# A convolution stage's in-order queues: table work in smaller pieces, moments and v's statistics at later steps

## The chip, the cores and the metric

The kernel runs on one core of a Trainium2 chip, in float32. The metric is the device time of one execution in microseconds (us); three executions of the kernel before took 2783.5, 2785.92 and 2796.28 us, with the median at 2785.92. The profile is of one further execution, whose instructions span 2780.5 us.

A core has engines that run beside one another, each through a queue of its own: TensorE (PE, and PEld for its weight loads), VectorE (DVE), ScalarE (ACT), GpSimd (POOL) and SyncE (SP), which here issues nearly all DMA transfers. They wait for one another through semaphores.

## The reference

The input x has 16 images of 16 channels, 256 by 256. There are two layers, each with a group norm ahead and a residual:

```python
x = x + _L0_conv_ref(_gn(x), L0_conv_weight)             # 3x3 circular convolution
x = x + _L1_conv_ref(_gn(x), ty, tx, poles1, poles2, residues)
```

The group norm takes mean and variance over groups of two channels of one image. The first layer is a circular 3x3 convolution, written with Fourier transforms in the reference. The second multiplies the spectrum of its input by tables that are made from complex poles and residues (terms like 1/(i omega - pole) along both axes), transforms back, and adds a transient part built from exp(pole t) and the same poles. The sum of x and the first layer is called v in the kernel; the second layer needs v's group norm, hence v's statistics.

## The kernel before

The program has three stages. The convolution stage reads x, forms v and stores it (vD). A second stage transforms v, mixes channels and stores spectra. A third one transforms back and writes the output. The change is in the first stage alone.

**The convolution stage.** One loop counts steps g from 0 to 386. An image takes 24 steps: four units of six steps, where a unit is a pair of row groups and the six steps are two phases by three taps. `conv(g)` issues 16 matmuls of 32 by 32 weights (32 in the trace) into ps_conv; row groups 2 and 3 run three steps behind 0 and 1. When a unit is complete, ScalarE evicts it into vt with the image's bias (line 266) and sums squares (line 274). VectorE later takes its moments (vst, line 268) and folds it (`mirror`, lines 231 and 232: vsum, then vt in place), and SyncE stores both.

**The row statistics of x** (`x_stats`) run one image ahead, as a generator that yields pairs of a due time and a piece of work. A due time d for image b means: run at step 24b - d. The pieces are sixteen `bn_stats` of x (line 166; the first eight on the image's first half of rows, the others on the second half), the aggregate (line 174), three tiny matmuls that spread a value over the channels of a group (`spread`, line 178, into ps_stat), with VectorE work between them: about_mean (lines 186 to 188), root (lines 194 and 195, the square root is on ScalarE), conv_weights (lines 154 to 157 and 202 to 211) and biases (lines 217 and 218). The buffer xq, which holds the aggregate and the bias, exists twice. ps_stat exists once.

**The loads of x.** Five buffers of half an image each. The first half of image b + 2 is loaded at step 3 of image b, the second at step 15.

**The tables** for the later stages are made beside the convolution by generators, one piece per call. One chain (poles, the two hat tables, the table c) is called at every second step, the other (the exponentials for both axes, then coef) at every fifth step. A hat table is made in two halves: loads from hD, squares on ScalarE (lines 425 and 426), a sum on GpSimd (428), a reciprocal of 512 columns (430), three multiplies on GpSimd (433), three VectorE operations (435, 437, 438), and four pairs of matmuls into ps_setup (448). Table c repeats eight times: GpSimd forms a denominator for two poles (571 to 573), VectorE inverts it (576), GpSimd builds weights (580) and multiplies (594), PE sums (607). An exponential piece: GpSimd forms an angle and its rounded number of turns (495 to 500), VectorE reduces the angle in three steps and clips it (506 to 508), ScalarE takes the sine (510), GpSimd multiplies and folds (512, 514).

**v's statistics** (`v_stats`) of images 0 to 11 are made in the stage as well, as the generator `early`: VectorE forms per-partition means, PE spreads them (line 322), VectorE goes on, PE sums (line 342), VectorE and ScalarE go on (lines 351 to 353), and a Newton step and a reciprocal finish vmr. Both matmuls use ps_stat. The generator is called at every third step from 297 on.

The order on each engine is the order in which this Python program issues the instructions: in a step first `conv(g)`, then `early`, the loads, the row statistics and the tables.

Of the kernel before, what the change touches and what calls it, by code (L numbers as in the profile page):

```python
# [16 lines left out]
B = 16  # L17
# [7 lines left out]
def conv_then_laplace_kernel(ctx: ExitStack, tc: tile.TileContext, a: dict, out: bass.AP):  # L25
# [15 lines left out]
    nc = tc.nc  # L41
# [93 lines left out]
    g128 = load1("g128", [P, P], tp)  # L135
# [23 lines left out]
    def x_stats(b):  # L159


        st = sp.tile([P, C, 6], FP, name="xst", tag="xst")

        def moments(j):
            r0 = 1 + 2 * (j % 8)
            nc.vector.bn_stats(st[:, j, :], halves[b][j // 8][:, r0 : r0 + 2, 1 : N + 1])  # L166

        for j in range(8):
            yield 38 - j, lambda: moments(j)
        for j in range(8, C):  # L170
            yield 33 - j // 2, lambda: moments(j)
        q = sp.tile([P, 12], FP, name="xq", tag="xq")
        mean, pvar, mu, d, e, var, sd, tmp, r, nb, bias = (q[:, j : j + 1] for j in range(11))
        yield 24, lambda: nc.vector.bn_aggr(q[:, 0:2], st)

        def spread(lhs, rhs):
            ps = pst.tile([P, 512], FP, name="ps_stat", tag="ps_stat")
            nc.tensor.matmul(ps[:, 0:1], lhsT=lhs, rhs=rhs, start=True, stop=True)
            return ps[:, 0:1]

        ps = []
        yield 18, lambda: ps.append(spread(g128, mean))

        def about_mean():

            nc.vector.tensor_copy(mu, ps[0])
            nc.vector.tensor_tensor(d, mean, mu, ALU.subtract)
            nc.vector.scalar_tensor_tensor(e, d, d, pvar, ALU.mult, ALU.add)

        yield 17, about_mean  # L190
        yield 14, lambda: ps.append(spread(g128, e))

        def root():
            nc.vector.tensor_scalar(var, ps[1], 1e-5, None, ALU.add)
            nc.scalar.activation(sd, var, AF.Sqrt)

        yield 12, root
        wc = sp.tile([P, 2, 3, 32], FP, name="wc", tag="wc")

        def conv_weights():  # L200
            newton(sd, var, tmp)
            nc.vector.reciprocal(r, sd)
            nc.vector.scalar_tensor_tensor(
                wc.rearrange("p h t m -> p (h t m)"),
                wband.rearrange("p h t m -> p (h t m)"),
                r,
                imask.rearrange("p h t m -> p (h t m)"),
                ALU.mult,
                ALU.add,
            )  # L210
            nc.vector.tensor_scalar(nb, mu, r, -1.0, ALU.mult, ALU.mult)

        yield 9, conv_weights
        yield 5, lambda: ps.append(spread(wsum.rearrange("p c m -> p (c m)"), nb))

        def biases():
            nc.vector.tensor_copy(bias, ps[2])
            nc.vector.tensor_scalar(shift[:, b : b + 1], mu, -1.0, None, ALU.mult)
            ready[b] = wc, bias

        yield 3, biases
# [171 lines left out]
    def make_hat(side):  # L393

        hatT = wp.tile([P, 6 * N], FP, name="hatT", tag="hatT")
        hatT = hatT[:, 0 : 2 * N].rearrange("p (j e t) -> p j e t", j=2, e=2)  # L400
        nc.sync.dma_start(out=hatT, in_=a[f"hatT{side}"])
        om = sw.tile([P, 3], FP, name="s_kcol", tag="s_kcol")
        nc.sync.dma_start(out=om[:, 0:1], in_=a["kcol"])
        om1, om2, scale = (om[:, j : j + 1] for j in range(3))
        to = ((tabE[:, 1:], tabO[:, :C]), (hB[:, 0], hB[:, 1]))[side]
        n = C * C * 2
        for half in range(2):
            tags = "s_re0", "s_re1", "s_pb", "s_im0", "s_im1", "s_den0", "s_den1"
            tiles = [
                sw.tile([P, 2 * n if t == "s_pb" else n], FP, name=t, tag=t)[:, 0:n] for t in tags  # L410
            ]
            pr, npi, m, sq, nb, g, b2 = tiles
            at = slice(half * n, half * n + n)
            for j in range(5):
                nc.sync.dma_start(out=tiles[j], in_=hD[j, side, at].partition_broadcast(P))
            yield
            yield
            if half == 0:
                omega(om1, om1, rd[:, side : side + 1])
                nc.vector.tensor_tensor(om2, om1, om1, ALU.mult)  # L420
                nc.vector.tensor_scalar(scale, cols[:, 17:18], -1.0, 1.0, ALU.mult, ALU.add)
                nc.vector.tensor_tensor(scale, scale, om1, ALU.add)
                nc.vector.tensor_scalar(hatT[:, 1], hatT[:, 1], scale, None, ALU.mult)
            yield
            nc.scalar.activation(g, sq, AF.Square, bias=om2)
            nc.scalar.activation(b2, nb, AF.Square)
            yield
            nc.gpsimd.tensor_tensor(g, g, b2, ALU.add)
            yield
            nc.vector.reciprocal(g, g)  # L430
            yield
            for z in (pr, npi, nb):
                nc.gpsimd.tensor_tensor(z, z, g, ALU.mult)
            yield
            nc.vector.scalar_tensor_tensor(sq, sq, om2, g, ALU.add, ALU.mult)
            yield
            nc.vector.scalar_tensor_tensor(pr, m, om2, pr, ALU.add, ALU.mult)
            nc.vector.scalar_tensor_tensor(npi, m, om2, npi, ALU.subtract, ALU.mult)
            for j, z in ((5, sq), (6, nb)):
                nc.sync.dma_start(out=z[0:1], in_=hD[j, side, at].unsqueeze(0))  # L440
            yield
            yield
            for eo in range(2):
                hv = to[eo].rearrange("p i (m r) -> p i m r", r=2)[:, 8 * half : 8 * half + 8]
                for ri, parts in enumerate(((pr, sq), (npi, nb))):
                    ps = psu.tile([P, 512], FP, name="ps_setup", tag="ps_setup")
                    for j, src in enumerate(parts):
                        nc.tensor.matmul(
                            ps, lhsT=hatT[:, j, eo], rhs=src, start=j == 0, stop=j == 1
                        )  # L450
                    yield
                    nc.scalar.copy(hv[:, :, :, ri], ps.rearrange("p (i m) -> p i m", i=8))
                    yield
# [24 lines left out]
    def make_exps(which):  # L478
# [10 lines left out]
        for q in range(8):  # L489
# [13 lines left out]
            c2 = float(np.float32(1.93500518798828125e-3))  # L503
            c3 = 2 * np.pi - c1 - c2
            for c in (c1, c2, c3):
                nc.vector.scalar_tensor_tensor(th, rn, -float(c), th, ALU.mult, ALU.add)
            nc.vector.tensor_scalar(th, th, phase, 3.1415925, ALU.add, ALU.min)
            nc.vector.tensor_scalar(th, th, -3.1415925, None, ALU.max)
            yield
# [14 lines left out]
    def make_c():  # L524
# [8 lines left out]
        z = space[:, 2 * N : 2 * N + 64].rearrange("p (j k) -> p j k", j=4)  # L533
# [30 lines left out]
        for k0 in range(0, C, 2):  # L564

            at = k0 // 2 % 2
            den = sw.tile([P, 2, N], FP, name="s_cden", tag=f"s_den{at}")
# [5 lines left out]
                nc.gpsimd.tensor_scalar(den[:, j], den[:, j], pr2[:, k : k + 1], None, ALU.add)  # L573
                nc.gpsimd.tensor_scalar(num[:, j], om, nm1, s0[:, k : k + 1], ALU.mult, ALU.add)
            yield
            nc.vector.reciprocal(den, den)
            w = sw.tile([P, 2, 4, 2, 4, 8], FP, name="s_w", tag=f"s_im{at}")
            for odd in range(2):
                for st in range(2):
# [10 lines left out]
                        ALU.mult,  # L590
                    )
            yield
            yield
            nc.gpsimd.tensor_tensor(num, num, den, ALU.mult)
            yield
# [2 lines left out]
            for i0 in range(0, 4, 2):  # L598
                c = c4[:, i0 : i0 + 2]
                ps = psu.tile([P, 2, N], FP, name="ps_setup", tag="ps_setup")  # L600
# [22 lines left out]
    def chain(*gens):  # L623
        for gen in gens:
            yield from gen
# [10 lines left out]
    for b in range(1, B):  # L636
        at_step.setdefault(max(0, 24 * b - 40), []).append((b, x_stats(b)))
    going = []
    tables = (
        (2, 0, chain(make_poles(), make_hat(0), make_hat(1), make_c())),  # L640
        (5, 1, chain(make_exps(0), make_exps(1), make_coef())),
    )
    early = v_stats(0, B - 4, lambda: pst.tile([P, 512], FP, name="ps_stat", tag="ps_stat"))
    for g in range(24 * B + 3):
        conv(g)
        if g > 24 * (B - 4) + 8 and g % 3 == 0:
            next(early, None)
        b, n = divmod(g, 24)
        if b + 2 < B and n == 3:
            halves[b + 2] = [load_x(b + 2, 0)]  # L650
        if b + 2 < B and n == 15:
            halves[b + 2].append(load_x(b + 2, 1))
        for b, gen in at_step.get(g, ()):
            going.append([b, gen, next(gen)])
        for it in list(going):
            while it[2] is not None and g >= 24 * it[0] - it[2][0]:
                it[2][1]()
                it[2] = next(it[1], None)
            if it[2] is None:
                going.remove(it)  # L660
        for every, first, gen in tables:
            if g % every == first:
                next(gen, None)
# [30 lines left out]
    m, n = cols[:, 16:17], cols[:, 17:18]  # L694
# [783 lines left out]
```

## Time and profile before

| | us |
|---|---|
| median of three executions | 2785.92 |
| span of the profile | 2780.5 |
| first convolution matmul starts | 26.1 |
| last convolution matmul ends | 638.2 |
| VectorE busy in the whole span | 1927.2 (69%) |
| PE busy in the whole span | 2614.0 (94%) |

The step at which each image starts on PE gives the images' durations, in us:

| image | 0 | 1 | 2 | 3 | 4 | 5 | 6 | 7 | 8 | 9 | 10 | 11 | 12 | 13 | 14 | 15 |
|---|---|---|---|---|---|---|---|---|---|---|---|---|---|---|---|---|
| us | 37.3 | 46.4 | 38.2 | 36.5 | 53.0 | 37.6 | 33.9 | 38.3 | 35.1 | 36.2 | 35.8 | 35.9 | 50.8 | 40.5 | 29.0 | 27.8 |

VectorE's larger groups in the stage: the moments of x 162.3 us (256 at 678 ns), the two parts of the fold 92.3 and 80.5 us (64 each, at 1442 and 1258 ns), v's moments 42.3 us (64 at 661 ns), the angle reduction's line 506 37.1 us (48 at 772 ns), and the twelve large reciprocals 26.7 us (eight at 3342 ns) and 13.4 us (four at 3338 ns).

A busy share is an average over a stage. To see what a stage waits for, the waits of each engine are read, and for each wait the instruction that stands at the head of the queue; all behind it on that engine waits too.

### The profile page before, as it was taken

What the parts mean: (1) busy time and instruction counts of PE and PEld (TensorE: products, weight loads), DVE (VectorE), ACT (ScalarE), POOL (GpSimd) and SP (SyncE); (2) the same over time, 40 slices, a digit from 0 to 9 for tenths busy, and PEclk for the clock granted to TensorE, in tenths of its full rate; (3) what the DMA queues carried; (4) which work ended last, traced back from release to release, by engine and by line L of the source; (5) the groups of instructions that cost most, each with busy time, mean ns of one, the idle gap of its engine ahead of it and who ended that gap; (6) DMA issues with size and microseconds to landing.
All of it is one profiled execution on the core that took longest, in us unless ns stands there. A gap on an engine that the chain in (4) does not pass through costs nothing.

```text
span 2780.5 us, 93064 instructions
## 1 busy us (share of the span) xinstructions
PE 2614.0 (94%) x39600; PEld 1956.3 (70%) x39600; DVE 1927.2 (69%) x3562; ACT 1524.6 (55%) x3093; POOL 1069.9 (38%) x989
## 2 busy tenths in 40 slices
PE   6878988798999999998999999999989999999998
PEld 3434444355777777775788888888778888888887
DVE  7888999867888888885444444544346667666666
ACT  4667778665666666664455555555434444444443
POOL 1543566502333333334111111111165656565653
PEclk9999999899999999999999999999999999999999
DMA  7777887655665556664666666666799989999995
GB/s 273 269 243 253 281 287 274 227 186 167 243 228 212 212 198 243 228 226 163 193 190 196 190 187 197 196 194 193 201 282 283 291 283 292 285 289 284 286 286 182
DMA packets 481199, 652.82 MB, mean 235 GB/s; under 512 B 51384, under 2 KB 459960, under 8 KB 466832
## 3 DMA queue, kind: packets, MB, share of 16 engines
q1 hardware_dynamic: 479712, 639.65, 71.1%
q8 instruction: 312, 5.11, 0.7%
q0 software_dynamic: 928, 3.02, 0.4%
q10 hardware_dynamic: 144, 4.19, 0.4%
q14 instruction: 103, 0.84, 0.1%
HBM read 367.22 MB, written 279.50 MB: 233 GB/s over the span
## 4 chain that ended last, share of the span: by engine, by line
PE 64%; DVE 13%; DMA 11%; POOL 4%; issue 4%; ACT 2%; SPq 2%; DVEq 0%; ACTq 0%; POOLq 0%
PE ps_mix L1050 16%; PE ps_s L984 9%; PE ps_y L732 8%; PE ps_y L740 8%; DMA yk<-yD 5%; PE ps_conv L249 5%; PE ps_x L775 4%; PE ps_p L1234 4%; PE ps_f L1258 3%; PE ps_f L1259 3%; DMA out_y<-ol 3%; DVE r L1267 2%; DVE xst L166 2%; PE psd L760 1%; SPq L1181 1%
## 5 line engine op out<-in xcount | busy, mean ns | idle before, releaser
L1050 PEld LDWEIGHTS ps_mix<-abd,sg 128*64 128x64 f32 x8192 | 447.7, 138 | 60.6 <-ACT sg L1107 49.0
L249 PE MATMUL ps_conv<-xt,wc 32*32 32x512 f32 x12288 | 463.6, 621 | 25.7 <-issue 22.6
L1050 PE MATMUL ps_mix<-abd,sg 128*64 128x128 f32 x8192 | 478.6, 275 | 8.6 <-ACT yt L1112 8.6
L1198 POOL TENSOR_TENSOR u<-yk 128x512 f32<-128x512 f32 (+1 forms) x268 | 345.4, 1320 | 311.7 <-PE ps_p L1234 204.3
L748 ACT ACTIVATE t<-ps_y,vmr 128x384 f32<-128x384 f32 x512 | 297.6, 582 | 163.0 <-PE ps_y L740 162.9
L249 PEld LDWEIGHTS ps_conv<-xt,wc 32*32 32x32 f32 x12288 | 232.1, 105 | 211.7 <-issue 137.3
L1112 DVE COPY yt<-ps_mix 128x512 f32<-128x512 f32 x128 | 88.5, 692 | 358.9 <-PE ps_mix L1050 232.6
L955 POOL TENSOR_TENSOR w<-v,mcol 128x2048 f32<-128x2048 f32 x32 | 115.6, 3613 | 562.5 <-DVE v L944 541.3
L732 PE MATMUL ps_y<-tabE,vq 128*128 128x256 f32 x1024 | 313.1, 387 | 8.7 <-DVE vq L721 7.1
L740 PE MATMUL ps_y<-tabO,vq 128*128 128x256 f32 x1024 | 305.9, 380 | 0.0
L1112 ACT COPY yt<-ps_mix 128x512 f32<-128x512 f32 x384 | 219.5, 588 | 153.1 <-PE ps_mix L1050 101.2
L1258 PE MATMUL ps_f<-pt,inv 128*128 128x256 f32 x1008 | 300.9, 380 | 0.0
L1259 PE MATMUL ps_f<-hs,ey 128*128 128x256 f32 x1008 | 299.9, 379 | 0.0
L1234 PEld LDWEIGHTS ps_p<-inv,u 128*128 128x128 f32 x2048 | 265.7, 193 | 46.1 <-issue 24.7
L1234 PE MATMUL ps_p<-inv,u 128*128 128x128 f32 x2048 | 279.1, 280 | 9.1 <-POOL u L1202 8.9
L1262 DVE TENSOR_TENSOR r<-ps_f,q 128x256 f32<-128x256 f32 x256 | 107.1, 418 | 249.8 <-ACT q L1261 249.8
L984 PE MATMUL ps_s<-ct,w 64*32 64x256 f32 x8448 | 261.2, 382 | 13.1 <-POOL w L952 12.2
L1107 ACT COPY sg<-ps_s 128x512 f32<-128x512 f32 x248 | 159.7, 645 | 182.8 <-PE ps_s L984 182.7
L1261 ACT COPY q<-ps_f 128x256 f32<-128x256 f32 x256 | 95.4, 373 | 285.1 <-PE ps_f L1259 283.6
L266 ACT ACTIVATE vt<-ps_conv,xq 128x512 f32<-128x512 f32 x256 | 167.2, 680 | 150.6 <-PE ps_conv L249 142.8
L732 PEld LDWEIGHTS ps_y<-tabE,vq 128*128 128x128 f32 x1024 | 189.5, 191 | 85.2 <-ACT q L788 50.3
L1236 ACT COPY pt<-ps_p 128x512 f32<-128x512 f32 x256 | 150.2, 587 | 134.7 <-PE ps_p L1234 119.2
(240 smaller groups left out, 4168.1 us busy)
## 6 DMA issues: line engine op xcount, KB each, us to landing
xt<-in_x SPq DMA_DIRECT2D x31, 2322.0 KB, 10.4
abd<-aD SPq DMA_DIRECT2D x512, 128.0 KB, 2.6
yD<-yt SPq DMA_DIRECT2D x512, 128.0 KB, 2.6
vl<-vD SPq DMA_DIRECT2D x256, 256.0 KB, 4.1
out_y<-ol SPq DMA_DIRECT2D x128, 512.0 KB, 9.4
s<-vD SPq DMA_DIRECT2D x252, 256.0 KB, 6.2
aD<-spec SPq DMA_DIRECT2D x15, 4096.0 KB, 12.5
yk<-yD SPq DMA_DIRECT2D x60, 1024.0 KB, 8.5
```

What stands on the lines that cost most here:

```text
L249: nc.tensor.matmul(acc[r][32 * c : 32 * c + 32], lhsT=ready[b][0][rows, phase, tap], rhs=halves[b][u // 2][rows, q : q + 5 : 4, 2 - tap : ...
L266: nc.scalar.activation(vt[:, r % 2], acc[r], AF.Identity, bias=ready[b][1], **by_sums)
L732: nc.tensor.matmul(ps[:, 0:N], lhsT=vf[:, xo, 0, j], rhs=tabE[:, 0 : i + 2 : i + 1], start=True, stop=False, skip_group_check=True,)
L740: nc.tensor.matmul(ps[:, P : P + N], lhsT=vf[:, xo, 1, j], rhs=tabO[:, i : C + 1 : C - i], start=False, stop=True, skip_group_check=True,)
L748: nc.scalar.activation(t[:, xo, j].rearrange("p l n -> p (l n)"), ps[:, 0:384], AF.Copy, scale=vmr[:, 0, b0 + j, i : i + 1],)
L984: nc.tensor.matmul(ps[odd][32 * iq : 32 * iq + 32, ro], lhsT=w[rows, iq, kk, ro], rhs=ct[rows, iq, kk], start=True, stop=True,)
L1050: nc.tensor.matmul(ps[64 * t : 64 * t + 64, j], lhsT=sg[:, f : f + 2].rearrange("p f m -> p (f m)"), rhs=abd[jq][:, :, 2 * t + cc, 2 * jj ...
L1112: (nc.vector.tensor_copy if m == 3 else nc.scalar.copy)(o, src)
L1198: nc.gpsimd.tensor_tensor(u[:, :, j].rearrange("p b (c n) -> p c b n", c=8), in0, in1, o)
L1234: nc.tensor.matmul(ps[:, at], lhsT=u[:, n], rhs=tab, start=True, stop=True)
L1258: nc.tensor.matmul(ps[:, e], lhsT=tab, rhs=pt[:, e], start=True, stop=False)
L1259: nc.tensor.matmul(ps[:, e], lhsT=ey[:, e], rhs=hs, start=False, stop=True)
```

## The change

The diff moves work between steps. The large reciprocals of the hat tables and of table c are cut into two of 256 columns, one step of their chain apart. The two last VectorE operations of a hat half are put into separate steps. The angle reduction is cut after its second operation, and the exponential chain is called at every fourth step for it. The second half's moments of x come three steps later, the aggregate two, the first spread and about_mean one; the second spread stays. v's statistics are called at six chosen steps in images 12 and 13 in place of every third step. The aim is that no long block of table work stands ahead of a short operation that another engine waits for, and that moments don't stand in the queue before their data are there.

```diff
         for j in range(8, C):
-            yield 33 - j // 2, lambda: moments(j)
+            yield 30 - j // 2, lambda: moments(j)
...
-        yield 24, lambda: nc.vector.bn_aggr(q[:, 0:2], st)
+        yield 22, lambda: nc.vector.bn_aggr(q[:, 0:2], st)
...
-        yield 18, lambda: ps.append(spread(g128, mean))
+        yield 17, lambda: ps.append(spread(g128, mean))
...
-        yield 17, about_mean
+        yield 16, about_mean
         yield 14, lambda: ps.append(spread(g128, e))
...
-            nc.vector.reciprocal(g, g)
-            yield
+            for z in (g[:, 0 : n // 2], g[:, n // 2 :]):
+                nc.vector.reciprocal(z, z)
+                yield
...
             nc.vector.scalar_tensor_tensor(pr, m, om2, pr, ALU.add, ALU.mult)
+            yield
             nc.vector.scalar_tensor_tensor(npi, m, om2, npi, ALU.subtract, ALU.mult)
...
                 nc.vector.scalar_tensor_tensor(th, rn, -float(c), th, ALU.mult, ALU.add)
+                if c == c2:
+                    yield
...
-            nc.vector.reciprocal(den, den)
+            nc.vector.reciprocal(den[:, 0], den[:, 0])
             w = sw.tile([P, 2, 4, 2, 4, 8], FP, name="s_w", tag=f"s_im{at}")
...
             yield
+            nc.vector.reciprocal(den[:, 1], den[:, 1])
             yield
             nc.gpsimd.tensor_tensor(num, num, den, ALU.mult)
...
-        (5, 1, chain(make_exps(0), make_exps(1), make_coef())),
+        (4, 1, chain(make_exps(0), make_exps(1), make_coef())),
...
-        if g > 24 * (B - 4) + 8 and g % 3 == 0:
+        if g - 24 * (B - 4) in (9, 14, 17, 38, 41, 44):
             next(early, None)
```

## The prediction

> **What bounds the kernel now.** I read the page first (it gives the span and the engines), then the busy time by stage, because an average over three stages with different limits says little. In the answer by stretches each row is a stretch in us, then busy time and instruction count of PE, PEld, DVE, ACT and POOL, then the granted TensorE clock:
>
> ```profile
> 0.00:26.11 26.11, 1.69 (x6) 1.51 (x6) 13.88 (x37) 1.49 (x2) 0.19 (x4) 1.00 0.87 334
> 26.11:638.15 612.04, 527.07 (x12703) 265.82 (x12702) 519.75 (x851) 435.39 (x1007) 273.92 (x252) 0.95 0.73 252
> 638.15:2780.50 2142.35, 2085.26 (x26893) 1688.97 (x26892) 1393.57 (x2674) 1087.72 (x2084) 795.80 (x733) 0.99 0.72 229
> ```
>
> The middle row is the convolution stage. Nothing else is touched by the diff, so the 2142 us after it are taken as fixed. In 612.0 us PE works 527.1 (86%) and VectorE 519.7 (85%): neither is saturated. They lose time to each other. 387 steps make 1.58 us a step.
>
> The same view cut at the images (24 steps each) shows where:
>
> ```profile
> 184.46:237.41 52.95, 38.90 (x806) 17.75 (x791) 44.40 (x68) 30.94 (x69) 17.78 (x13) 0.90 0.67 206
> ...
> 418.49:454.29 35.80, 31.98 (x822) 16.01 (x812) 33.40 (x52) 28.57 (x67) 21.14 (x22) 0.95 0.77 275
> ...
> 490.16:540.93 50.77, 34.73 (x827) 16.29 (x807) 45.31 (x81) 28.58 (x66) 31.61 (x36) 0.83 0.61 213
> 540.93:581.38 40.45, 32.12 (x823) 15.91 (x814) 32.66 (x52) 28.62 (x70) 5.82 (x4) 0.92 0.68 227
> ```
>
> Image 11 (second row) is an ordinary one: VectorE works 33.4 of 35.8 us and bounds it. Images 4 and 12 take 15 us more. So the time to win lies in a few disturbed images and not in all sixteen.
>
> Then the waits, each engine alone, from 60 to 582 us (us in total, times, longest). First VectorE's, then PE's:
>
> ```profile
> DVE xst L166 <- DMA xt<-in_x: 18.4, 6, 7.8
> DVE xq L174 <- ACT vt L266: 13.6, 4, 6.1
> DVE vsum L231 <- ACT vt L266: 12.2, 8, 2.6
> DVE s_th L506 <- POOL s_rn L500: 4.0, 2, 2.2
> DVE s_cden L576 <- POOL s_cden L573: 3.1, 2, 2.1
> ```
>
> ```profile
> PE ps_stat L178 <- DVE xq L174: 13.7, 5, 6.5
> PE ps_stat L322 <- DVE xq L194: 10.4, 1, 10.4
> PE ps_stat L178 <- DVE xq L188: 10.3, 3, 6.8
> PE ps_stat L178 <- DVE vmr L353: 5.1, 1, 5.1
> ```
>
> Last the timeline (start, duration, engine, line, what, and in brackets the idle time before it with what ended it), for three of these:
>
> ```profile
> 183.72 1.29 DVE L166 BATCH_NORM_STATS2 xst<-xt 128x6 f32<-128x512 f32 x2 [7.80 <-DMA xt<-in_x]
> 241.12 0.59 DVE L174 BATCH_NORM_AGGREGATE xq<-xst 128x2 f32<-128x96 f32 x1 [6.08 <-ACT vt L266]
> 514.93 0.60 PE L322 MATMUL ps_stat<-vs,g 128*128 128x12 f32 x2 [10.44 <-DVE xq L194]
> ```
>
> The first is the second half of an image that is not yet in SBUF. The second is the aggregate, which overwrites a buffer whose bias ScalarE still needs. The third is v's mean at step 300, which needs the one ps_stat bank, and that bank is read by the root (L194), which stands behind 3 us of sine reduction and other work in VectorE's queue.
>
> **What the Trainium skill says.** "PSUM — Partial Sum Buffer", section "Engine vs sequencer instructions", has the queues of ScalarE, VectorE and GpSimd as strict FIFO, and matmuls starting in program order. The trace agrees: for the 10.44 us ahead of 514.93 no convolution matmul runs, though its data are there. "TensorE: Matmul & The Clock Gate", section "HAM oscillation — how this bites in real kernels", wants no PE gaps above some 3.4 us, or the clock falls. The image with the 10.44 us gap has 0.83, image 6 (274.99 to 308.91, without such a gap) has 1.00; these losses are inside the durations above, so I don't add them again. "Vector Engine (DVE) Microarchitecture Reference", section "5.2 Measured stream behaviour on trn2", gives about 75 ns fixed cost an instruction; I use it once.
>
> **The change, part by part.** Waits by event are from the VectorE timeline.
>
> Second-half moments go 3 steps later (4.7 us). Their load is issued at step 15 of an image and takes 10.4 us (page, part 6); the first moment came 4 steps (6.3 us) after it and now comes 7 steps (11.1 us) after. Of the six waits on loads, four are on second halves: 2.55, 7.80, 0.47 and 4.07 us, 14.9 in sum. Cut by 4.7 each, 3.1 of the 7.8 stays. Gain 12. First halves (1.67 and 1.79) are not helped.
>
> The aggregate goes 2 steps later (3.2 us). It stood at step 0 of the image and needs the evictions that step 2 issues; now it stands behind them. Waits 4.06, 6.08, 0.40 and 3.04 become 0.9, 2.9, 0 and 0: 9.8 saved on paper. But vsum at step 4 needs the same evictions, so part returns as L231 waiting. I credit half: 5.
>
> v's statistics. Before: pieces at steps 9, 12, 15, 18, 21, 24 of image 12, between the row statistics' own uses of the one ps_stat bank (steps 6, 10, 19). Step 12 needs the root, itself at step 12, and the third spread at 19 needs v's read at 21, which stands two steps behind it. Those are the 10.44 and 5.07 us. After: 9, 14, 17 of image 12 and 14, 17, 20 of image 13, and every use of the bank comes two steps behind the last read. Some 15.5 us of PE waiting go. VectorE sets how much of that is time: some 2 us of its work (L351, L353 and the first reciprocal) also moves from image 12 (45.3 busy) to 13 (32.7). With 3 us idle in each, 43.3 + 3 and 34.7 + 3 make 84.0 against 91.2, 7.2 less; the 4.07 and the 3.04 above lie in the same two images and are partly this gain, so I credit 6, not 7.2.
>
> Reciprocals in two halves and sine reduction in two pieces: no work is saved. The half of s_cden needs only the GpSimd work of its own half, so the 3.1 us of waiting go: 3. Shorter blocks in the queue serve the waits on L174 and L188; nothing more credited.
>
> Gains 12 + 5 + 6 + 3 = 26 us.
>
> Costs. Twelve more instructions at 75 ns: 1. The sine chain: its rate stays (4 pieces of 5 steps become 5 of 4), but from one sine to the next reduction there are 12 steps and not 15, 4.7 us less for GpSimd. The timeline's sixteen reductions now have 0 to 24 us between L500's end and L506's start; five have less than 4.7 (0.0, 0.0, 1.3, 3.0, 4.3), which would lack 14.9 in all. The phase against the other tables moves, so between 0 and 14.9 I take 4. The second spread now follows about_mean by 2 steps, not 3; behind it on PE wait all convolution matmuls, then ScalarE. From image 8 on, by the timeline's ends of L188, VectorE was done between 0.6 us before and 6.7 us after PE arrived there, so each such image gains about one step of VectorE's work (33.8/24 = 1.4 us) of PE waiting, some 10 in all; but PE has 36 - 32 = 4 us to spare in these, and VectorE has later work queued. Between 0 and 10 I take 2.5. The multiply behind the second reciprocal (POOL L594, then PE L607) comes 1.5 us later (2 steps less half a reciprocal of 3.34 us); three of eight have only 0.1 to 0.8 us of room: 4 us of PE waiting, I take 1. The table loads at steps 84 and 120 go to 92 and 132. The first leaves the x load of step 87 alone (good), the last now stands ahead of the one of step 135: 1.5. Sum 1 + 4 + 2.5 + 1 + 1.5 = 10.
>
> Net 26 - 10 = 16: 2785.9 - 16 = **2770 us**. The tables end at step 356 and not 345, in images 14 and 15, where VectorE has room (20.6 busy of 29.0 in image 14): nothing.
>
> **Rivals.** (1) The wait changes places. PE and VectorE both have some 14% to spare, and what is taken from one comes back on the other: L174 becomes L231, the 10.4 us become several waits at L188. For it: spreads 2 are already late from image 8 on. Against it: the two ps_stat waits are caused by the order itself. Only the load waits pay, 12, with 8 of costs: 2782. (2) The tighter chain is worse. If the sine chain lacks all 14.9 us, the spreads cost their 10, and 4, 1 and 4 come from the other terms, costs are 34; with the gains 26, 2785.9 + 8 = 2794. For it: GpSimd works 60 to 70% in images 7 to 12. Against it: three quarters of the reductions have room.
>
> **How the numbers follow.** Forecast 60%, rival 1 28%, rival 2 12%. Forecast's own spread is some 8 us each way. Faster by 0.5% means under 2772: 0.45 from the forecast and 0.03 from a mild rival 1, 0.48. Slower by 0.5% means over 2799.8: most of rival 2's upper half, 0.08. The rest is 0.44. All gains without costs, and the vsum half returned as well, give 2785.9 - 30 = 2756; I take 2756 as the low end and 2790 as the high, which leaves out most of rival 2.
>
> **What would show it.** Right: the stage ends near 622 us; no wait of PE at v's mean above 3 us; image 4 near 43 and image 12 near 46; VectorE's waits for x loads below 7 us. Wrong: more than 10 us of VectorE waiting for s_rn, L188's waits on PE at 20 us or more, or ordinary images (7 to 11) above 37 us, which would mean that the short distances cost more than the long blocks did.

## The result, and the profile after

The changed kernel takes 2772.52 us (median of six executions, 2766.67 to 2778.56), the kernel before 2787.26 us in the same series. The ratio is 0.9944, with a 95% interval of 0.9922 to 0.9965: about 15.6 us faster. The forecast was 2770 us, 16 us faster.

The busy time by stage, after (stretch in us; busy time and instruction count of PE, PEld, DVE, ACT and POOL; granted clock; DMA share and rate):

```profile
0.00:26.11 26.11, 1.63 (x6) 1.46 (x6) 13.90 (x37) 1.49 (x2) 0.19 (x4) 1.00 0.86 335
26.11:625.72 599.61, 522.00 (x12703) 266.99 (x12703) 509.71 (x863) 433.96 (x1006) 268.43 (x252) 0.95 0.74 256
625.72:2764.90 2139.18, 2086.59 (x26892) 1690.67 (x26892) 1393.04 (x2674) 1088.11 (x2084) 793.52 (x733) 0.99 0.72 229
```

The convolution stage went from 612.0 to 599.6 us. The rest went from 2142.4 to 2139.2, without any change in it, so 12.4 of the 15.6 us between the two profiled spans are the stage's. Each kernel has one profile, and the rest is not steady: in the fourteen profiles of this case it took 2139.2 to 2150.3 us, though no edit touches it. A difference of a few us between two whole times need therefore not lie in the stage.

The same view cut at images 4, 6, 11 and 12 of the changed kernel (each stretch holds the 768 convolution matmuls of one image):

```profile
185.44:229.28 43.84, 34.35 (x798) 17.05 (x799) 36.87 (x61) 29.30 (x65) 18.52 (x13) 0.92 0.73 246
...
267.16:314.52 47.36, 37.37 (x805) 17.84 (x799) 35.43 (x60) 27.39 (x63) 21.06 (x15) 0.93 0.67 239
...
448.81:486.25 37.44, 31.82 (x823) 15.51 (x816) 32.69 (x52) 28.82 (x71) 22.57 (x24) 0.95 0.74 260
486.25:528.64 42.39, 34.93 (x825) 17.06 (x822) 38.67 (x71) 30.04 (x70) 29.77 (x29) 0.88 0.74 262
```

Images 4 and 12 fell by 9 and 8 us, though both are still longer than an ordinary image. But image 6, which took 33.9 us before, now takes 47.4, nearly as long as the disturbed images did, and image 3 went from 36.5 to 41.7. So the change eased two disturbances and made a new one.

Part of the reason shows in the waits between 60 and 582 us (total, times, longest). VectorE's:

```profile
DVE vsum L231 <- ACT vt L266: 15.0, 8, 2.6
DVE s_th L508 <- POOL s_rn L502: 13.6, 6, 4.1
DVE xq L174 <- ACT vt L266: 8.2, 3, 4.6
```

PE's (from the old L430 on, lines stand a few further down in the changed kernel; L508 is the old L506, L502 the old L500; L174 is the aggregate, and L188 is the last line of about_mean, for which the second spread waits):

```profile
PE ps_stat L178 <- DVE xq L188: 26.1, 9, 6.6
...
PE ps_stat L178 <- DVE xq L174: 9.8, 8, 3.1
```

The 18.4 us of waiting for loads of x are gone altogether, and so are PE's waits of 10.4 us at v's mean and 5.1 us behind vmr. In their place VectorE waits 13.6 us for s_rn (4.0 before), and PE waits 26.1 us for about_mean (10.3 before). The timeline of image 6, in VectorE's, PE's and GpSimd's rows, shows how these two hang together:

```profile
273.19 1.28 POOL L434 TENSOR_TENSOR s_im<-s_im,s_den 128x512 f32<-128x512 f32 x1
...
280.99 1.49 POOL L502 TENSOR_SCALAR s_rn<-s_rn 128x512 f32<-128x512 f32 x1
...
282.51 1.42 DVE L508 SCALAR_TENSOR_TENSOR s_th<-s_rn,s_th 128x512 f32<-128x512 f32 x2 [2.97 <-POOL s_rn L502]
...
285.76 0.59 PE L178 MATMUL ps_stat<-xq,g 128*128 128x1 f32 x2 [6.60 <-DVE xq L188]
```

GpSimd finishes the hat table's multiplies (L434) and only then makes the angle (8 us, to 282.5). VectorE stands 2.97 us at the head of its queue for it. about_mean stands behind that, and PE stands 6.6 us for about_mean with the image's convolution matmuls behind it. This wait is about half of the 13.5 us by which image 6 grew. VectorE also has more to do in this image than before, 35.4 us against 29.9, which the new steps of the table pieces may have put there.

### The profile page after: what moved, and what is told of

The parts are those of the page before. It is cut to its first block, busy times and chain, and to the rows that moved or that the text cites. A ratio compares the mean times of both kernels' runs of the same rounds, so it can differ in the third digit from the quotient of the medians.

```text
span 2764.9 us, 93061 instructions
## 1 busy us (share of the span) xinstructions
PE 2610.2 (94%) x39600; PEld 1959.1 (71%) x39600; DVE 1916.6 (69%) x3574; ACT 1523.6 (55%) x3092; POOL 1062.1 (38%) x989
## 4 chain that ended last, share of the span: by engine, by line
PE 65%; DVE 13%; DMA 9%; POOL 4%; issue 4%; ACT 2%; SPq 2%; DVEq 0%; ACTq 0%; POOLq 0%
PE ps_mix L1055 16%; PE ps_s L989 9%; PE ps_y L737 8%; PE ps_y L745 8%; PE ps_conv L249 4%; PE ps_x L780 4%; DMA yk<-yD 4%; PE ps_p L1239 4%; PE ps_f L1263 4%; PE ps_f L1264 4%; DMA out_y<-ol 3%; DVE r L1272 2%; DVE xst L166 2%; PE psd L765 1%; DVE ol L1274 1%
## 5 line engine op out<-in xcount | busy, mean ns | idle before, releaser
L249 PE MATMUL ps_conv<-xt,wc 32*32 32x512 f32 x12288 | 456.5, 622 | 17.7 <-issue 11.3
L989 PE MATMUL ps_s<-ct,w 64*32 64x256 f32 x8448 | 261.0, 381 | 13.1 <-POOL w L957 12.2
```

Source lines behind the costliest of these rows:

```text
L249: nc.tensor.matmul(acc[r][32 * c : 32 * c + 32], lhsT=ready[b][0][rows, phase, tap], rhs=halves[b][u // 2][rows, q : q + 5 : 4, 2 - tap : ...
L989: nc.tensor.matmul(ps[odd][32 * iq : 32 * iq + 32, ro], lhsT=w[rows, iq, kk, ro], rhs=ct[rows, iq, kk], start=True, stop=True,)
```

## The experiments

Each ratio is to the kernel before, timed on the same chip; intervals are at 95%. Three theories stood at the start: the prediction's sum of parts (in the expectations: the theory of the prediction); its rival 1, that only the load waits pay; and a third, that the new steps of the hat loads make the gain. The first three kernels take one group of edits each, the fourth takes the first two groups together.

**v's statistics alone.** Edit, on the kernel before:

```diff
-        if g > 24 * (B - 4) + 8 and g % 3 == 0:
+        if g - 24 * (B - 4) in (9, 14, 17, 38, 41, 44):
```

> Before, with v's statistics alone at the new steps (9, 14, 17 of image 12 and 14, 17, 20 of image 13). Theory of the prediction: the 10.4 and 5.1 us of PE waiting at ps_stat go and VectorE gives back 6 us: ratio to before near 0.998. Rival 1 (only the load waits pay, a PE wait that goes comes back at another place): 1.000. A third theory, that the phase of the table loads makes the difference: 1.000. In the trace: image 12 under 46 us in the first theory, still about 50 in the others.

Measured: 0.9970 (0.9958 to 0.9983), 8.4 us. Image 12 went from 50.8 to 40.4 us. The wait behind vmr is gone, but v's mean still holds PE for 7.3 us here (10.4 before). Rival 1 gave this part nothing, and it falls here.

**The row statistics alone.** Edit: `33 - j // 2` to `30 - j // 2`, and due times 24, 18, 17 to 22, 17, 16.

> Before, with the row statistics of x alone at the new steps (second-half moments 3 later, aggregate 2, first spread and about_mean 1). Theory of the prediction: 12 us from the load waits, 5 from the aggregate, minus 2.5 for the second spread, so about 14 us: ratio 0.995; VectorE's waits for x loads fall from 18 to about 7 us. Rival 1: 12 from the loads, lost in part again: 0.997. Third theory (the 7.8 us wait comes from the hat loads of step 84 that stand ahead of the x load, not from the moments' place): the 7.8 us wait mostly stays, ratio 0.998.

Measured: 0.9939 (0.9925 to 0.9953), 17 us. No wait of VectorE for a load of x is left between 60 and 570 us (14.3 us before), although the hat loads stand where they stood. The third theory falls with this.

**The table pieces alone.** Edit: all parts of the diff that concern the hat tables, table c and the exponentials.

> Before, with the table pieces alone (reciprocals in halves, hat operations apart, angle reduction in two, exponentials every fourth step). Theory of the prediction: 3 us gained at s_cden, 7 us of costs, so 4 us slower: ratio 1.0015; VectorE waits some 10 us for s_rn, and v's mean still holds PE for about 10 us. Rival 1: 1.000. Third theory (the phase of the table loads decides): faster, 0.996 or less, with the 7.8 us load wait gone although the moments stand where they stood.

Measured: 1.0026 (1.0015 to 1.0036), 7 us slower. Images 1 and 6 take 54.4 and 51.6 us here (46.4 and 33.9 before). VectorE's and PE's waits of this kernel, 60 to 570 us:

```profile
DVE xq L174 <- ACT vt L266: 23.1, 8, 7.7
DVE s_th L508 <- POOL s_rn L502: 17.6, 5, 5.0
...
DVE xst L166 <- DMA xt<-in_x: 11.9, 5, 5.6
```

```profile
PE ps_stat L178 <- DVE xq L188: 31.7, 8, 10.1
...
PE ps_stat L178 <- DVE vmr L353: 5.0, 1, 5.0
...
PE ps_stat L322 <- DVE xq L194: 1.0, 1, 1.0
```

The wait behind vmr is as before (5.1 us): smaller pieces don't help a wait that the order of uses of one bank makes. The wait at v's mean (L322) is another matter. It was expected to stay near 10 us, and it fell from 10.4 to 1.0, more than v's own new steps alone took from it. So that wait came mostly from what stood ahead of the root in VectorE's queue, and less from the order of the bank's uses. The s_rn wait (4.0 before), the longer waits at L174 (13.6 before) and those at L188 (10.3 before) come with this part.

**The table work put back.** Edit: the kernel after, without those parts.

> After, with the table work put back as it was before, so that the row statistics and v's statistics alone are moved. Theory of the prediction: the sum of these two parts, 6 + 14 us: ratio to before 0.993, a little faster than after. Rival 1: 0.997. Third theory: most of the gain is lost, 0.998, since the table loads stand at their old steps.

Measured: 0.9922 (0.9909 to 0.9934), 22 us. The two helpful parts alone make 8.4 + 17 = 25 us, together 22. With the 7 us of the tables, the three parts add to 18 us, where the whole change brought 15.6. The stage of this kernel's profile:

```profile
26.11:621.24 595.13, 532.64 (x12702) 267.93 (x12697) 519.65 (x851) 434.07 (x1006) 273.23 (x252) 0.96 0.75 259
```

VectorE is busy for 519.7 us of it and idle for 75.5. In the kernel before it is busy for 519.8 us and idle for 92.3, in the changed kernel busy for 509.7 and idle for 89.9. So the table pieces shorten VectorE's busy time by 10 us, though they save no work (5.5 us of it at L232, 94.5 to 89.0), and lengthen its holes by 14.

So a third of the diff works against the rest. The next kernels take that third apart, on the base of the last one (0.9922). Theory A: the sine pieces cost, through s_rn. Theory B: the hat pieces cost, through their new steps.

**Plus the sines.** Edit on the base: the cut after c2, and the chain's `(5, 1,` to `(4, 1,`.

> Base is the kernel with the row statistics and v's statistics moved and all table work as before (0.9922 of before). Added here: the angle reduction in two pieces with its chain at every fourth step. Theory A, formed on the runs so far: this piece is the one that costs, since GpSimd has 12 and not 15 steps from a sine to the next reduction and VectorE stands at the head of its queue until s_rn is done, ahead of about_mean: VectorE waits for s_rn over 10 us, PE waits at L188 over 20 us, ratio 0.9945 or more. Theory B (the hat pieces cost, by their new steps against the images): no s_rn waits beyond 4 us, ratio 0.9925.

Measured: 0.9953 (0.9939 to 0.9967), 8.6 us worse than the base. The cost is as theory A has it, the mechanism is not:

```profile
DVE s_cden L578 <- POOL s_cden L575: 8.1, 6, 3.8
...
DVE s_th L506 <- POOL s_rn L500: 3.2, 1, 3.2
```

The wait for s_rn is 3.2 us, below the kernel before's, and PE waits 6.6 us at L188. VectorE's wait for table c's denominators grew instead, to 8.1 us where the base has 3.8. GpSimd does both, so the sines' new steps may have put it late for the denominators; that these 4 us are the cost is not shown. In the two profiles the stage is 599.4 us against the base's 595.1, and another 9.5 us lie behind it, where nothing was edited.

**Plus the hats.** Edit on the base: the reciprocal of g in two halves, and one more `yield` after pr.

> The same base, added: the hat tables' reciprocal in two halves and their last two operations in separate steps, so that a half takes 20 pieces and not 18. Theory A: no cost beyond 1 us, ratio 0.992 to 0.9925. Theory B: the halves now fall on other images and stand against the x loads of step 135: ratio 0.9945 or more.

Measured: 0.9929 (0.9914 to 0.9943), 2 us worse, which the intervals don't separate. But the images change places: 1 to 6 take 250.7 us (the base 239.8), 7 to 11 take 172.0 (179.7). A hat half lasts 40 steps instead of 36, so table c begins 16 steps later, its work leaves image 7, and images 14 and 15 take 61.3 us (56.7). PE waits 23.1 us at L188 here without the sine pieces, and image 6 takes 47.7 us, so both come with the hats. The meeting of image 6 stands in this trace too: GpSimd's hat multiplies, then the angle, then VectorE's whole sine reduction ahead of about_mean, and 5.8 us of PE waiting for it.

**Plus the halves of c.** Edit on the base: `reciprocal(den, den)` to `den[:, 0]`, and `den[:, 1]` one piece later.

> The same base, added: the reciprocal of table c in two halves. Both theories: VectorE's 3.8 us of waiting for s_cden mostly goes, PE waits up to 4 us more for s_num; ratio 0.991 to 0.9925. If this piece were the cost, 0.9945.

Measured: 0.9905 (0.9884 to 0.9926), 4.7 us better than the base, within the intervals. The s_cden wait is gone from VectorE's list; PE waits 9.0 us for s_num instead, which costs nothing that the time shows.

**The aggregate alone.** Edit on the kernel before: due times 24, 18, 17 to 22, 17, 16, without the moments.

> The kernel before with the aggregate two steps later, the first spread and about_mean one step later, and the second half's moments where they stood. Prediction's terms: 5 us from the aggregate minus 2.5 for the second spread, ratio 0.999, with VectorE's waits for x loads still near 18 us. If the moments' place gives nothing and the aggregate all: 0.994.

Measured: 1.0000 (0.9990 to 1.0010). VectorE still waits for the loads:

```profile
DVE xst L166 <- DMA xt<-in_x: 16.4, 6, 6.8
DVE xq L174 <- ACT vt L266: 10.2, 3, 5.6
```

So the 17 us of the row statistics need the moments' move; the later aggregate, first spread and about_mean show no gain by themselves. The moments' move without them was not run.

On this base the long waits for s_rn come from neither part alone (3.9 us with the hats, 3.2 with the sines, 13.6 in the changed kernel, which has both). Theory R: a hat half now lasts 40 steps, twice the 20 of a sine, so that the same collision on GpSimd comes back in each hat half. Two kernels take one side away, one shifts the phase, and a last one tries the lost step between about_mean and the second spread.

**The sines at another phase.** Edit on the kernel after: `(4, 1,` to `(4, 3,`.

> After, with the sine chain called at steps 3, 7, 11 ... and not 1, 5, 9 ..., so that each reduction stands two steps later against the hat pieces. Theory R (resonance): after's waits for s_rn come from the hat half's period of 40 steps, twice the sine's 20, so that GpSimd has the hat multiplies directly ahead of the same part of every second sine: with the shift VectorE's 13.6 us of s_rn waits fall below 7 and the time to 0.991 or 0.992. Theory N (the sine pieces cost wherever they stand): no change, 0.994 to 0.9955.

Measured: 0.9942 (0.9924 to 0.9959), as after.

```profile
DVE s_th L508 <- POOL s_rn L502: 6.4, 3, 3.7
```

The wait halves as theory R has it, but the time, for which it named 0.991 or 0.992, doesn't move. L188 holds PE for 21.4 us still, and vsum (L231) waits 21.5 us where it waited 15.0. Image 6 takes 44.6 us, though PE's wait at L188 in it fell from 6.6 to 3.0. So the time doesn't follow the s_rn wait; whether its loss was made up elsewhere, at vsum for one, is not shown.

**The hats put back.** Edit: the kernel after without the diff's two parts on the hats.

> After, with the hat pieces put back as they were (18 pieces a half). If the parts simply add: f1 plus the gain of the halves of c, 0.9936. Theory R: the resonance goes with the 40-step halves, s_rn waits near 3 us, 0.991.

Measured: 0.9927 (0.9908 to 0.9945). L188 holds PE for 3.0 us and image 6 takes 34.0 us. PE waits 15.2 us for s_num, and images 7 to 11 take 186.0 us (171.7 after). The waits go with the hat pieces, as theory R has it. The time doesn't decide, since the interval holds both 0.991 and the 0.9936 of parts that add.

**The sines put back.** Edit: the kernel after without the diff's two parts on the sines.

> After, with the angle reduction whole and its chain at every fifth step. If the parts simply add: 0.9912 (base, hats and halves of c). Theory R: the same 0.991, with s_rn waits of 4 us. If the hats' own waits (6 us at L188 in images 1 and 6) were after's cost: 0.994.

Measured: 0.9946 (0.9931 to 0.9962), as after. With the hat pieces in, the sine pieces cost nothing more; without them they cost 8.6 us. And the hats, 2 us on the base, cost 11 us once the halves of c are in (0.9946 against 0.9905, intervals apart). By these times the table parts don't add (the sum named 0.9912), and the third case named, that the hats' own waits cost, has the time right with 0.994. The profiles don't bear it out inside the stage: it takes 594.9 us here and 594.0 without the hats, and the part behind it, which is the same in both, takes 2148.3 and 2141.0. What the hats lose in images 1 to 6 (4.2 us) they more than win back in images 7 to 11 (10.4 us).

**The second spread a step later.** Edit, on the base with the halves of c:

```diff
-        yield 14, lambda: ps.append(spread(g128, e))
+        yield 13, lambda: ps.append(spread(g128, e))
```

> The best kernel so far (row statistics and v's statistics moved, reciprocals of c in halves, 0.9905) with the second spread at due time 13 and not 14, so that three steps lie between about_mean and it, as in the kernel before. The prediction's term (2.5 us for the lost step): 0.9895 and PE's 4.9 us of waiting at L188 mostly gone. If the lost step costs nothing: 0.9905.

Measured: 0.9895 (0.9875 to 0.9916), 2759.69 us. This is faster than the kernel before by 29 us, and its interval lies below that of the kernel after (0.9922 to 0.9965). Against 0.9905 without this edit it is not separated in time, so a gain from it is not shown. In the profiles PE's wait at L188 fell from 4.9 us to 3.3, and the stage is 594.0 us without the edit and 585.0 us with it, more than that wait explains:

```profile
26.11:611.10 584.99, 526.09 (x12703) 263.01 (x12702) 520.62 (x859) 433.15 (x1007) 275.89 (x252) 0.96 0.76 263
```

VectorE is busy 89% of this stage, against 85% in both the kernel before and the kernel after. Against the kernel before the gain is just that: the same work (520.6 us busy) with fewer holes (64.4 us idle against 92.3).

## Why the prediction was right, by its own steps

The total was right, and the gains were right in their main causes. The parts are as follows.

- **Second-half moments and aggregate: 12 + 5 - 2.5 = 14.5 us forecast, 17 us measured** (row statistics alone). The step about the loads was right in cause and sign, and too careful: 4.7 us later was enough even for the 7.8 us wait, where 3.1 us of it were expected to stay, and the two waits on first halves (1.67 and 1.79 us), which were held not to be helped, went too; why they all went was not isolated. The 5 us for the aggregate found no support. With the second spread's cost, 2.5 us were forecast for the aggregate's kernel; it gives 0, with an interval of 2.8 us either way, which just reaches the forecast. The wait at L174 fell only from 13.6 to 10.2 us, where 3.8 was expected to stay. The other half was to come back at vsum (L231), but that wait fell as well, from 12.2 to 6.9, and vst's (L268) for the same evictions grew from 3.7 to 7.9.
- **v's statistics: 6 us forecast, 8.4 us measured.** The mechanism, uses of one bank in a wrong order, holds for the wait behind vmr: 5.1 us, gone with these steps alone, unmoved by the table pieces. For the longer wait at v's mean it holds in part. That fell to 7.3 us with these steps, to 4.4 with the row statistics as well, and it is gone in the changed kernel only with the table pieces, which alone bring it to 1.0. The prediction had named the long block ahead of the root in VectorE's queue, but credited the 10.4 us to the order. That 6 us came out near is in part luck.
- **Tables: 3 us gained and 7.5 us of costs forecast, 4.5 us worse; 7 us worse measured.** The sine term was set at 4 us out of 0 to 14.9. VectorE's wait for s_rn grew by 9.6 us, so the step from slack to wait was near two thirds of its upper end. The time does not follow that wait, as the shifted phase shows. The waits at L188 came by a way that was not priced: the hats' new steps, which had a term for their loads alone. Whether they are what the tables cost is open, since the hats alone cost 2 us within noise. The halves of c were set at a gain of 3 and a cost of 1; measured 4.7, within noise. Twelve more instructions were set at 1 us with 75 ns from the Trainium skill, "Vector Engine (DVE) Microarchitecture Reference", section "5.2 Measured stream behaviour on trn2"; two halves of 1718 ns for one of 3342 ns make 94 ns, 1.1 us in all.
- **The lost step between about_mean and the second spread: 2.5 us forecast for 10 us of PE waiting.** With the row statistics alone PE waits 7.5 us at L188, less than the 10.3 before, so the lost step by itself made no such wait. In the changed kernel 12.8 of the 26.1 us are two waits in images 1 and 6, and 11.2 us are five waits from image 8 on, near the 10 that were forecast there. Both go when the hats are put back (3.0 us in all). The prediction had the shorter blocks as a help at L188; it looked at the hats' loads and not at where their pieces meet about_mean. Giving the step back (the last experiment) brings 2.8 us, near the 2.5 set and within noise.

Of the signs named beforehand, the right ones came: the stage ends at 625.7 us (622 named), v's mean holds PE no longer, image 4 takes 43.8 us (43 named) and image 12 42.4 (46 named), no load wait is left. Two of the wrong ones came as well: s_rn above 10 us and L188 above 20. The third did not: images 7 to 11 average 34.3 us and not above 37, although the waits at L188 came there too, while images 1 and 6 are the ones that grew or stayed long. That table c's later start relieved images 7 to 11 fits this, but it was not isolated. So two errors met. The row and v's statistics brought 22 us together and not 20.5, and the tables took back some 6 and not 4.5. Each of these differences is inside the intervals of the single parts (about 3 to 4 us either way), so that the total came out within 1 us is luck. One reading of the second rival's is a little off: GpSimd's share in images 7 to 12, given as 60 to 70%, is 55 to 74% in the view by images.

Open is the interplay of the table pieces: why the hats cost 2 us on one base and 11 on the other, and the sines 8.6 on one and nothing on the other. Since the profiles put 4.1 of the 8.6 us and 0.9 of the 11 into the stage, it is open too how much of this interplay is in the stage at all; several profiles of each kernel would tell. That the hat, sine and c pieces share GpSimd's queue is shown by their waits; which meeting sets the time was not isolated. Two sets of s_th and s_rn, so that GpSimd need not wait for the sine before the next angle, were not tried.

## What to carry to other kernels

In a hand-ordered kernel with in-order queues, first move an operation to behind the arrival of its data, and bring all uses of a single bank into an order in which each read stands ahead of the next use; each paid alone here (17 and 8.4 us). Cutting long blocks into pieces is another matter: it changes the steps of everything behind them in the chain, and what it then meets decides: here the same pieces took away the wait at v's mean and made another at about_mean. Make each group of edits alone before judging the sum, since here the last third of the change cost 6 of the 22 us that the others had brought. And look at the part that no edit touches: what it varies by from profile to profile is the least that a single profile's total can be off.

## What the runs showed of the hardware that was not expected

A reciprocal of 128 by 512 took 3342 ns and its half 1718 ns, so halving one added only about 0.1 us; a tensor_tensor of twice the size (L231, 128 by 1024) took 1258 ns.

The length of some VectorE operations is not fixed; it depends on what GpSimd runs beside them. The subtraction of v's means (L326, 128 by 12, two inputs) took 1.07 us in the kernel before, from 517.36 to 518.43 us, while GpSimd's L512 ran from 517.13 to 518.40; in the changed kernel it took 0.17 us with the same operands, while GpSimd ran L497, which has one tensor input where L512 has two. This is not a single case. The small tensor_tensors of the row statistics (L155, L156 and L187) began inside a GpSimd tensor_tensor 90 times in the fourteen traces, with a median of 0.69 us, and inside a GpSimd tensor_scalar 177 times, with a median of 0.16 us, the same as with GpSimd idle. The second part of the fold (L232, 128 by 1024) took 1.22 to 1.23 us in all 411 cases without GpSimd, and 1.89 us on average, at most 2.33, where a GpSimd tensor_tensor ran beside more than half of it. The moments of x (L166) took 0.63 to 0.70 us in either case. So where a piece of GpSimd's work is put changes VectorE's busy time too.
